# Summing each unit's products three units behind its scan, and a convolution in two halves of 64 columns

## The chip, the cores and the metric

The kernel runs on one core of one Trainium2 chip. The metric is the device time of one launch in microseconds (us); the time given for a kernel is the median of its runs. The core has five engines that run side by side and wait for each other through semaphores: TensorE (PE; its weight loads are shown apart, as PEld), VectorE (DVE), ScalarE (ACT), GpSimd (POOL) and SyncE (SP), which here issues the DMAs.

## The reference

Four layers of a selective scan over images, each added to its input, `x = x + layer(_gn(x))`. `_gn` normalises groups of three channels. x has 8 images of 48 x 48 pixels and 96 channels. A layer, cut to what matters:

```python
xz = x @ in_proj_w.T                                   # 96 -> 2 x 192 channels
xc, z = jnp.split(xz, 2, axis=-1)
xc = conv 3x3, each of the 192 channels alone; xc = silu(xc + conv_b)
xs = [xc by rows, xc by columns, both of them backwards]          # K = 4 directions
dts, Bs, Cs = split(einsum('bkdl,kcd->bkcl', xs, x_proj_w))       # Bs, Cs: 16 states
delta = softplus(einsum('bkrl,kdr->bkdl', dts, dt_proj_w) + bias)
def step(h, inp):                                      # over the 2304 pixels
    h = exp(delta * A) * h + (delta * u) * B           # h: 192 channels x 16 states
    y = sum over states of h * C
y = sum of the four directions + D * xs; y = layernorm(y) * silu(z)
return y @ out_proj_w.T
```

Layers 0, 1 and 2 are of this form. Layer 3 writes the same recurrence with cumulative sums and a division by the decay; the kernel shortens it to the ends of each direction as long as the decay has died out, and a check at the end decides whether it must be done in full.

## The kernel before

**Work and order.** The images are taken in four pairs, layer after layer, so there are 16 passes (layer l, pair p). The 192 channels of two images make three tiles of 128 partitions (t = 0 and 1: 128 channels of one image; t = 2: the last 64 channels of both). In layers 0 to 2 a pass has 12 groups (tile, row or column order `ph`, direction `d`), each group three scans of 768 pixels (class `Chunk`, lines 684 to 875), each scan 16 *units*. Unit n takes two states (n // 2 and n // 2 + 8) of 64 channels at once, 128 partitions. That makes 3 x 4 x 12 x 3 x 16 = 6912 units. Layer 3 uses class `Edge` (lines 877 to 995), four units to a group, four states to a unit, 192 pixels: 192 units.

**A unit of layers 0 to 2.** Its steps, with the engines:

- `load` (743): SP loads C's two rows into a `cb` buffer [128, 768], spread over 64 partitions each (`fetch`, 718, DMA at line 724); at n = 0 also `brow`, the B rows in bf16 (749).
- `decay` (756, `exp` at 761): ACT makes exp(delta x A) into a `da` tile (line 764).
- `spread` (769): PE spreads B from `brow` over the partitions into the PSUM tile `b` (line 667), of which there are two buffers (`pb`).
- `scan` (786): DVE multiplies b by du (line 794) and runs the recurrence (line 798); POOL multiplies the C buffer by the result (line 807).
- In six units of 16 (n = 2, 5, 7, 10, 13, 15, `pooled`, 709) B is loaded by DMA into a `bb` buffer (`load_b`, 731) and multiplied by du on POOL (`weigh`, line 741); ACT then writes the decay into the PSUM tile `b` (764 by way of line 777).
- `add_up` (844): PE adds the products over the states into the PSUM accumulator `acc` (line 854, weights `twin`, two halves of 64 columns). A call for unit n treats one half of the pixels of the pair of units it belongs to; with the second half the two cb buffers come free. At n = 1 `begin_sum` (825) starts the accumulator (line 839, from the y so far); the last call, `add_up(NS)` from `rest_of_sum` (1194), comes with the first unit of the next scan and hands `collect` (863) to a list, which the next unit carries out: ACT copies acc to y (line 871).

**What sets the order.** `run` (1170) writes the order out by hand: for unit k it calls `get_ready(k + 1)` (1199), which issues `load_b` for k + 5, `load` for k + 4, `spread` for k + 1, `weigh` and `decay` for k + 3; then the scan of k; then `add_up` for k - LAG, with LAG = 2 (line 1167), the lag of the sum behind the scan. `keep_order` (1156) fixes that order on every engine for layers 0 to 2. Beside it run side tasks, one step per unit (`beside`, 1264): `coming` (`prepare`, 580: delta and delta x u for the next scan: lines 603, 611 to 617, 623, `to_twins` with ACT copies at 578, the DVE product at 631 or 634), and either `behind` (`epilogue`, 998, of the pass before) or `ahead` (`prologue`, 287, of the next pass). In the unit where the lagging sum is at n = 0 (`ends`, 1270) no step of `behind` or `ahead` is taken. `ahead` begins at unit LAG of a pass (1239).

**The prologue** normalises, projects the input (line 404 for 128 channels, 413 for the other 64), and convolves (`convolve`, 302): for each of 5 chunks of up to 480 pixels nine matmuls of a diagonal 128 x 128 weight `diag` with the shifted, padded image `pad` (line 312) into one PSUM bank, then an ACT copy (320). A step is one of the nine matmuls. There are 16 x 3 x 5 x 9 = 2160 of these. An f32 matmul stands as two records (two passes) in the trace.

**Constants.** `cst` [128, 352] holds the identity, a 128 x 128 block of 1/192 (`mean_w`) and the group matrix; ACT negates `mean_w` into `off` (line 173).

Of the kernel before, what the change touches and what calls it, by code (L numbers as in the profile page):

```python
# [39 lines left out]
F32 = mybir.dt.float32  # L40
BF16 = mybir.dt.bfloat16
AF = mybir.ActivationFunctionType
# [7 lines left out]
P = 128  # L50
NB, H, W, DM = 8, 48, 48, 96
L = H * W
DIN = 192
# [50 lines left out]
def ss2d_layers_kernel(ctx: ExitStack, tc: tile.TileContext, x_in, consts, weights, out):  # L104
    nc = tc.nc

    cpool = ctx.enter_context(tc.tile_pool(name="const", bufs=1))
# [3 lines left out]
    ddpool = ctx.enter_context(tc.tile_pool(name="dd", bufs=2))  # L111
    ypool = ctx.enter_context(tc.tile_pool(name="y", bufs=1))
    rpool = ctx.enter_context(tc.tile_pool(name="brow", bufs=2))
    cbpool = ctx.enter_context(tc.tile_pool(name="cb", bufs=9))
    bbpool = ctx.enter_context(tc.tile_pool(name="bb", bufs=3))
    apool = ctx.enter_context(tc.tile_pool(name="da", bufs=4))
    capool = ctx.enter_context(tc.tile_pool(name="carry", bufs=2))
# [8 lines left out]


    nc.scalar.preload_act_table_set("natural_log_exp_and_others")
    cst = cpool.tile([P, 2 * P + DM], F32, name="cst")
    nc.sync.dma_start(cst, consts)  # L130
    ident = cst[:, 0:P]
    mean_w = cst[:, P : 2 * P]
    group_w = cst[0:DM, 2 * P : 2 * P + DM]
    ones = cpool.tile([P, 1], F32, name="ones")
    nc.gpsimd.memset(ones, 1.0)
    minus = cpool.tile([P, 1], F32, name="minus")
# [33 lines left out]


    off = cpool.tile([P, P], F32, name="off")
    nc.scalar.activation(off, mean_w, AF.Copy, scale=-1.0)
    off_2 = cpool.tile([P, 2, P], F32, name="off_2")
    off_22 = cpool.tile([P, P], F32, name="off_22")
    for b in range(2):
# [91 lines left out]
    def silu(o, i, **kw):  # L268

        with tc.issue_after(nc.scalar.activation(o, i, AF.Silu, **kw).ins):  # L270
            nc.scalar.preload_act_table_set("natural_log_exp_and_others")

    def bank():
        return psum.tile([P, BANK], F32, name="ps", tag="ps")
# [8 lines left out]


    GATED, READY = "gated", "ready"

    def prologue(l, p, short=False, first=False):
        ly = layers[l]
# [13 lines left out]
        def convolve(pad, t):  # L302

            while place["tiles"] < t and not first:
                yield GATED
            u[t] = upool.tile([P, L], F32, name=f"u_{l}_{p}_{t}", tag="u")
            for c0, m in CHUNKS:
                r0, nr = c0 // W, m // W
                ps = bank()
                for j in range(9):  # L310
                    dy, dx = divmod(j, 3)
                    nc.tensor.matmul(  # L312
                        ps[:, :m],
                        ly.diag[:, int(t == 2), j, :],
                        pad[:, r0 + dy : r0 + dy + nr, dx : dx + W],
                        start=(j == 0),
                        stop=(j == 8),
                    )
                    yield True
                nc.scalar.activation(  # L320
                    u[t][:, c0 : c0 + m], ps[:, :m], AF.Identity, bias=ly.column(t, C_CONVB)
                )
                yield
            silu(u[t], u[t])
            yield
# [6 lines left out]
        for b in range(2):  # L332
            x = tmp.tile([DM, L], F32, name=f"x_{l}_{p}_{b}", tag="tmp")
            if l == 0:
# [14 lines left out]
                for i, (c0, m) in enumerate(CHUNKS):  # L349
                    q, ld = m // 4, loaded[i]  # L350
                    ps = bank()
# [27 lines left out]
            ps = bank()  # L379
# [8 lines left out]
            ps = bank()  # L388
            nc.tensor.matmul(ps[0:DM, 0:1], group_w, dv, start=True, stop=True)
            yield True  # L390
            scale, shift = gn[:, b, 0:1], gn[:, b, 1:2]
# [6 lines left out]
            pad = padded(f"pad_{l}_{p}_{b}")  # L398
            q0 = 64 * b
            for c0, m in CHUNKS:  # L400
                r0, nr = c0 // W, m // W
                rows = slice(1 + r0, 1 + r0 + nr)
                ps = bank()
                nc.tensor.matmul(
                    ps[:, :m], ly.inw[:, 0:P], x[:, c0 : c0 + m], start=True, stop=True
                )
                yield True
                nc.scalar.copy(
                    pad[:, rows, 1 : W + 1], ps[:, :m].rearrange("p (r w) -> p r w", w=W)
                )  # L410
                yield
                ps = bank()
                nc.tensor.matmul(
                    ps[q0 : q0 + 64, :m], ly.inw[:, P:DIN], x[:, c0 : c0 + m], start=True, stop=True
                )
                yield True
                nc.scalar.copy(
                    pad2[q0 : q0 + 64, rows, 1 : W + 1],
                    ps[q0 : q0 + 64, :m].rearrange("p (r w) -> p r w", w=W),
                )  # L420
                yield
# [742 lines left out]
                last[i.engine] = i.name  # L1164

    groups = [(t, ph, d) for t in range(3) for ph in range(2) for d in range(2)]
    LAG = 2
    LOADS, DECAYS = 3, 2

    def run(pairs, short):  # L1170
# [58 lines left out]
        for k, ((l, p, unit), c, n) in enumerate(todo):  # L1229
# [7 lines left out]
            if done:  # L1237
                behind, done = Side(epilogue(*done), 195), None
            if unit == LAG and following:
                ahead = Side(begin(*following), 300)  # L1240
# [28 lines left out]

            ends = l not in short and k > LAG and todo[k - LAG][2] == 0  # L1270
            if busy and l not in short:
                beside()
            if k >= LAG:
                (bl, bp, _), b, bn = todo[k - LAG]
                rest_of_sum(k - LAG)
                if bl in short:
                    collected()
                b.add_up(bn)
                if k > LAG and todo[k - LAG - 1][0][:2] != (bl, bp):
                    done = todo[k - LAG - 1][0][:2]  # L1280
# [20 lines left out]
    ps = bank()  # L1301
# [100 lines left out]
```

## Time and profile before

| what | value |
|---|---|
| median of 3 runs | 20514.42 us (20494.02 to 20516.52) |
| the profiled execution | 20509.65 us, span 20507.7 us |
| busy share PE, PEld, DVE, ACT, POOL | 84%, 37%, 86%, 79%, 87% |
| mean granted PE clock | 0.904 |
| POOL product L807, mean of one | 1.817 us and 1.815 us |
| DVE scan L798, mean of one | 1.739 to 1.814 us by form |
| DVE product L794, mean of one | 0.946 us |
| PE sum L854, busy in all | 7018.1 us in 27648 records |
| PE convolution L312, busy in all | 2165.7 us in 4320 records |

How to read it: "busy" is the time in which an engine executed something. A group's row names the line, the engine, the operation, what it writes and reads, the shape, the count, then busy time, mean duration of one in ns, and the engine's idle time just before these instructions with what ended it. The list of waits says which engine and line waited for which, in total, how often, and the longest. In the timeline a row is a run of like instructions: start, length, engine, line; a matmul's end is modelled, so the next row's start tells more than its length. The granted clock of PE is a share of full speed.

### The profile page before, as it was taken

Reading aid. Unit: us, or ns where it says so; the run is one execution under the profiler, and the core shown is the slowest. Engines: PE = TensorE matmul, PEld = TensorE weight load, DVE = VectorE, ACT = ScalarE, POOL = GpSimd, SP = SyncE. Lnnn points to the kernel's source line nnn. Section 1 sums busy time; section 2 is a strip of 40 time slices with the busy share of each in tenths; the row PEclk is TensorE's granted clock in tenths of the full one; section 3 lists DMA queues with packets and bytes.
Section 4 is the critical chain, followed back from the end, with each engine's and each line's share of the span. In section 5 each row is a group of like instructions: output and inputs, shape, how many; then the busy total and the mean of one; then the engine's idle time right before and its main releaser. Section 6 shows DMA issues by size and latency. Waiting matters only on the chain. (4 is left out here: it accounts for less than half of the span.)

```text
span 20507.7 us, 304889 instructions
## 1 busy us (share of the span) xinstructions
PE 17283.2 (84%) x88322; PEld 7546.6 (37%) x88322; DVE 17656.0 (86%) x14161; ACT 16243.7 (79%) x30020; POOL 17768.2 (87%) x10121
## 2 busy tenths in 40 slices
PE   8888888888888888888888888888888888888886
PEld 2323333333333333333333333333333333335565
DVE  5999999999999999999999999989989989995543
ACT  5777887887887887887877887877877877877776
POOL 5999999999999999999999999999999999995432
PEclk8998998998998999998998999988988998999997
DMA  5888888888888888888888888888888888883221
GB/s 147 223 221 222 219 220 224 222 219 221 220 225 222 219 229 221 221 229 219 221 228 220 217 225 219 218 218 220 217 219 219 220 219 222 219 220 109 76 72 51
DMA packets 1963444, 4200.13 MB, mean 205 GB/s; under 512 B 369456, under 2 KB 720048, under 8 KB 1948592
## 3 DMA queue, kind: packets, MB, share of 16 engines
q1 hardware_dynamic: 1961776, 4180.52, 77.8%
q8 instruction: 726, 11.89, 0.3%
q14 instruction: 942, 7.72, 0.2%
HBM read 4026.64 MB, written 152.27 MB: 204 GB/s over the span
## 5 line engine op out<-in xcount | busy, mean ns | idle before, releaser
L807 POOL TENSOR_TENSOR cb<-cb,da 128x768 f32<-128x768 f32 x4320 | 7831.3, 1817 | 799.5 <-issue 258.3
L854 PE MATMUL acc<-cb,twin 128*64 128x384 f32 x27648 | 7018.1, 542 | 663.6 <-POOL cb L807 660.3
L798 DVE TENSOR_TENSOR_SCAN da<-da,carry,b 128x768 f32<-128x768 f32 x2880 | 5223.3, 1814 | 176.4 <-ACT b L764 2.3
L741 POOL TENSOR_TENSOR bb<-bb,du 128x768 f32<-128x768 f32 x2592 | 4714.0, 1819 | 361.0 <-DMA bb<-xd 207.8
L794 DVE TENSOR_TENSOR b<-du,b 128x768 f32<-128x768 f32 x4320 | 4087.6, 946 | 883.9 <-PE b L667 785.4
L807 POOL TENSOR_TENSOR cb<-cb,bb 128x768 f32<-128x768 f32 x2592 | 4705.1, 1815 | 155.0 <-DVE bb L798 57.1
L667 PE MATMUL b<-brow,pick 96*64 96x512 bf16 (+2 forms) x18816 | 2761.6, 355 | 1787.6 <-DVE da L798 1408.4
L764 ACT ACTIVATE da<-dl,a 128x768 f32<-128x768 f32 x4320 | 4013.6, 931 | 245.8 <-POOL cb L807 214.0
L854 PEld LDWEIGHTS acc<-cb,twin 128*64 128x64 f32 x27648 | 2268.9, 150 | 3089.4 <-issue 1400.3
L798 DVE TENSOR_TENSOR_SCAN bb<-b,carry,bb 128x768 f32<-128x768 f32 x1728 | 3109.0, 1799 | 114.8 <-ACT b L764 53.5
L764 ACT ACTIVATE b<-dl,a 128x768 f32<-128x768 f32 x2592 | 2334.4, 901 | 590.2 <-DVE da L798 558.4
L798 DVE TENSOR_TENSOR_SCAN da<-da,b 128x768 f32<-128x768 f32 x1440 | 2525.4, 1754 | 85.6 <-DVE b L794 0.9
L667 PEld LDWEIGHTS <-pick 96*64 96x64 bf16 x18816 | 974.1, 114 | 4192.1 <-DVE da L798 2506.3
L578 ACT COPY dl<-ps 64x384 f32<-64x384 f32 x3456 | 1635.3, 473 | 756.7 <-PE ps L623 720.7
L312 PE MATMUL ps<-pad,diag 128*128 128x480 f32 (+1 forms) x4320 | 2165.7, 599 | 11.5 <-DVE eyc L1087 9.9
L623 PE MATMUL ps<-du,cst 128*64 128x384 f32 (+1 forms) x7296 | 1709.7, 516 | 93.1 <-ACT du L617 77.0
L578 ACT COPY du<-ps 64x384 f32<-64x384 f32 x3456 | 1635.7, 473 | 190.0 <-DVE ps L634 91.2
L798 DVE TENSOR_TENSOR_SCAN bb<-b,bb 128x768 f32<-128x768 f32 x864 | 1502.2, 1739 | 94.9 <-ACT b L764 40.5
L623 PE MATMUL ps<-dl,cst 128*64 128x384 f32 (+1 forms) x7296 | 1412.4, 483 | 0.0
L312 PEld LDWEIGHTS ps<-pad,diag 128*128 128x128 f32 x4320 | 687.5, 191 | 1211.4 <-issue 1090.1
L603 PE MATMUL ps<-dts,w 6*128 6x384 f32 (+5 forms) x2432 | 946.3, 595 | 176.1 <-DMA dts<-xd 103.7
L611 ACT ACTIVATE du<-ps,w 128x384 f32<-128x384 f32 (+1 forms) x912 | 521.4, 572 | 622.3 <-PE ps L603 611.5
(144 smaller groups left out, 19159.8 us busy)
## 6 DMA issues: line engine op xcount, KB each, us to landing
cb<-xd SPq DMA_DIRECT2D x13952, 192.0 KB
bb<-xd SPq DMA_DIRECT2D x5184, 192.0 KB
brow<-xb SPq DMA_DIRECT2D x864, 72.0 KB
yd<-y SPq DMA_DIRECT2D x48, 1152.0 KB
ey<-yd SPq DMA_DIRECT2D x256, 216.0 KB
cb<-xd SPq DMA_DIRECT2D x128, 384.0 KB
ex<-xs SPq DMA_DIRECT2D x256, 108.0 KB
xd<-xt SPq DMA_DIRECT2D x32, 684.0 KB
```

The costliest lines, as they stand in the source:

```text
L312: nc.tensor.matmul(ps[:, :m], ly.diag[:, int(t == 2), j, :], pad[:, r0 + dy : r0 + dy + nr, dx : dx + W], start=(j == 0), stop=(j == 8),)
L578: nc.scalar.copy(z[64 * h : 64 * h + 64, g, at], v[64 * g : 64 * g + 64])
L603: nc.tensor.matmul(o[:, :m], ly.dtw[q0 : q0 + r, k, chans], dts[q0 : q0 + r, at], start=True, stop=True,)
L611: nc.scalar.activation(e, v, AF.Abs, bias=bias)
L623: nc.tensor.matmul(v[half], ident[:, half], z1, start=(i == 0), stop=(i == 3))
L667: nc.tensor.matmul(o[64 * h : 64 * h + 64], pick[:, b, n : n + 1].to_broadcast([2 * NR, 64]), rows, start=True, stop=True,)
L741: nc.gpsimd.tensor_mul(b, b, self.du[n % 2])
L764: nc.scalar.activation(da, self.dl[n % 2], AF.Exp, scale=layers[self.l].a2[:, int(self.t == 2), n % 2, k, i : i + 1],)
L794: nc.vector.tensor_mul(b, self.du[n % 2], b)
L798: nc.vector.tensor_tensor_scan(way(h), way(da), way(b), start, ALU.mult, ALU.add)
L807: nc.gpsimd.tensor_mul(c, c, h)
L854: nc.tensor.matmul(self.acc[64 * g : 64 * g + 64, a, : self.m // 2], twin, c[:, a, :], start=False, stop=(pair + 2 == NS and not self.turns),)
```

## The change

Three things in one diff. The sum of a unit is issued three units behind its scan instead of two (`LAG = 3`), with ten `cb` buffers instead of nine. Each convolution matmul of 128 output columns, and the input projection's, becomes two matmuls of 64 columns that write the two halves of the partitions of the same PSUM bank; a step of the convolution holds both. The constants tile loses the block of 1/192, is loaded by two DMAs, and `off` is set by a POOL memset. Everything else stands as before; lines from 286 on move down by one to three.

```diff
-    cbpool = ctx.enter_context(tc.tile_pool(name="cb", bufs=9))
+    cbpool = ctx.enter_context(tc.tile_pool(name="cb", bufs=10))
...
-    cst = cpool.tile([P, 2 * P + DM], F32, name="cst")
-    nc.sync.dma_start(cst, consts)
+    cst = cpool.tile([P, P + DM], F32, name="cst")
+    nc.sync.dma_start(cst[:, 0:P], consts[:, 0:P])
+    nc.sync.dma_start(cst[0:DM, P:], consts[0:DM, 2 * P :])
     ident = cst[:, 0:P]
-    mean_w = cst[:, P : 2 * P]
-    group_w = cst[0:DM, 2 * P : 2 * P + DM]
+    group_w = cst[0:DM, P:]
...
-    nc.scalar.activation(off, mean_w, AF.Copy, scale=-1.0)
+    nc.gpsimd.memset(off, -1.0 / DIN)
...
+    halves_of = [slice(64 * g, 64 * g + 64) for g in range(2)]
...
                 for j in range(9):
                     dy, dx = divmod(j, 3)
-                    nc.tensor.matmul(
-                        ps[:, :m],
-                        ly.diag[:, int(t == 2), j, :],
-                        pad[:, r0 + dy : r0 + dy + nr, dx : dx + W],
-                        start=(j == 0),
-                        stop=(j == 8),
-                    )
+                    for half in halves_of:
+                        nc.tensor.matmul(
+                            ps[half, :m],
+                            ly.diag[:, int(t == 2), j, half],
+                            pad[:, r0 + dy : r0 + dy + nr, dx : dx + W],
+                            start=(j == 0),
+                            stop=(j == 8),
+                        )
                     yield True
...
-                nc.tensor.matmul(
-                    ps[:, :m], ly.inw[:, 0:P], x[:, c0 : c0 + m], start=True, stop=True
-                )
+                for half in halves_of:
+                    nc.tensor.matmul(
+                        ps[half, :m], ly.inw[:, half], x[:, c0 : c0 + m], start=True, stop=True
+                    )
...
-    LAG = 2
+    LAG = 3
```

## The prediction

> **What bounds the kernel now.** I read the page's busy line first, then the stretch without the start and the short last layer, then the waits, then the order on PE. The busy line and clock row of the page:
>
> ```profile
> PE 17283.2 (84%) x88322; PEld 7546.6 (37%) x88322; DVE 17656.0 (86%) x14161; ACT 16243.7 (79%) x30020; POOL 17768.2 (87%) x10121
> ...
> PEclk8998998998998999998998999988988998999997
> ```
>
> ```profile
> 600.00:18460.00 17860.00, 15147.65 (x76202) 6204.17 (x76199) 16311.59 (x12272) 14371.34 (x26559) 16594.10 (x9416) 0.91 0.85 221
> 18460.00:20508.00 2048.00, 1653.99 (x10282) 1168.22 (x10279) 981.14 (x1609) 1503.15 (x2789) 804.23 (x480) 0.89 0.28 77
> ```
>
> The columns of the second are PE, PEld, DVE, ACT, POOL busy, clock, DMA share, GB/s. In layers 0 to 2 (first line) POOL is busy 92.9% and DVE 91.3%: two engines with nearly the same load, each feeding the other. POOL's idle time there is 17860 - 16594 = 1266 us, and no edit that leaves POOL's work as it is can gain more. The short layer 3 (second line) saturates nothing.
>
> ```profile
> L807 POOL TENSOR_TENSOR cb<-cb,da 128x768 f32<-128x768 f32 x4320 | 7831.3, 1817 | 799.5 <-issue 258.3
> ...
> L741 POOL TENSOR_TENSOR bb<-bb,du 128x768 f32<-128x768 f32 x2592 | 4714.0, 1819 | 361.0 <-DMA bb<-xd 207.8
> L794 DVE TENSOR_TENSOR b<-du,b 128x768 f32<-128x768 f32 x4320 | 4087.6, 946 | 883.9 <-PE b L667 785.4
> ```
>
> A scan of 16 units costs POOL 16 x 1.817 + 6 x 1.819 = 40.0 us; it takes 17860 / (6725/16) = 42.5 us. What POOL waits for is blurred ("issue"), so I paired each of the 6912 L807 rows with its unit's scan L798: 1042 of them came after an idle POOL and began within 0.35 us of that scan's end, 928 us in all. POOL runs dry when DVE is late, and DVE is late mostly for b:
>
> ```profile
> PE b L667 <- DVE da L798: 1408.4, 1025, 6.0
> ...
> DVE b L794 <- PE b L667: 785.4, 745, 5.9
> ...
> PE acc L854 <- POOL cb L807: 660.3, 506, 8.8
> ...
> ACT y L871 <- PE acc L854: 295.0, 276, 6.3
> ```
>
> ```profile
> SPq L724 <- PE acc L854: 2065.0, 1769, 6.1
> ```
>
> So there is a ring: PE takes its queue in order; L854, a unit's sum, waits for POOL; behind the sum of unit k-3 stands L667, which makes b for unit k+1; DVE waits for b; POOL then waits for DVE. I followed PE back from each of DVE's waits for b in layers 0 to 2 to PE's last idle time: 326 of them (366 us) start at an L854 that waits for L807, most at unit 11 of a scan, where the pooled units 7 and 10 have put POOL behind. The rest start elsewhere and pass through full stretches of PE. What fills PE there is seen in its timeline (start, length):
>
> ```profile
> 8033.08 0.54 PE L854 MATMUL acc<-cb,twin 128*64 128x384 f32 x1 [2.13 <-POOL cb L807]
> ...
> 8038.75 0.81 PE L854 MATMUL acc<-cb,twin 128*64 128x384 f32 x4
> 8039.40 1.46 PE L623 MATMUL ps<-dl,cst 128*64 128x384 f32 x8
> 8040.69 0.49 PE L667 MATMUL b<-brow,pick 96*64 96x512 bf16 x4
> 8041.01 0.81 PE L854 MATMUL acc<-cb,twin 128*64 128x384 f32 x4
> 8041.76 1.07 PE L312 MATMUL ps<-pad,diag 128*128 128x480 f32 x2
> 8042.76 0.87 PE L854 MATMUL acc<-cb,twin 128*64 128x384 f32 x4
> 8043.55 1.07 PE L312 MATMUL ps<-pad,diag 128*128 128x480 f32 x2
> ```
>
> Read starts, not lengths: L854 takes 0.65 us before a 64-column L623 but 0.75 before the 128-column convolution L312 and 0.79 between two of them; L312 itself takes 1.00.
>
> **The skill.** The Trainium skill, "TensorEngine Tiling (Array Packing)", Key Properties, says that changing the tiling mode drains TensorE and that different tiles compute in parallel. The trace agrees with both: 0.10 us appears ahead of a change of width, and eight 64-column records of 384 columns (four pairs, L623) take 1.29 us, 0.32 per pair. "TensorE: Matmul & The Clock Gate", Part 2, says that weight loads are pulled ahead while matmuls stay in order: hence the ring above. Part 1 of that page says that PE's clock halves when it has been idle for a window of about 3.4 us and returns after a busy one. The trace's clock records agree in kind: 608 stretches at half clock, 3927 us, in multiples of 3.41 us; but it drops after windows that were 40% busy too.
>
> **The change part by part.** All against the profiled execution, 20509.65 us (span 20507.7); the median of the runs, 20514.42, stands 5 us above.
>
> (1) *LAG 3.* At unit k PE now sums unit k-3, which POOL was given one unit (2.65 us) earlier. The wait of 660 us on PE mostly goes; POOL's lag behind the scan's end is 1.2 us in the median and 3.6 us at the 95th percentile. For DVE I take, wait by wait, the smaller of DVE's wait and the L854 wait at its root: 302 us. Take 300. Bounds: 0, if another buffer holds DVE back; 366, if the whole stretch goes. Ten buffers: the load issued at unit k takes the buffer of k-6 instead of k-5; in both cases the sum that frees it is issued at k-1 at the latest, so SP's loads wait no longer than before, and each add-up asks for an older product. What is late next is ACT's decay L764, which waits for POOL to free one of four da tiles (see the rivals).
>
> (2) *Convolution in pairs.* Two passes of 480 columns at 0.32 x 480/384 make 0.805 us for 1.00; the L854 ahead saves 0.10, the next one about 0.05 (a following L667 0.02). That is 0.33 us per matmul. Of 2160 matmuls 1620 (3240 rows of two passes) lie in layers 0 to 2: 535 us of PE. L404 adds 120 x 0.3 = 36. In the short layer convolutions run one after the other, where passes already start 0.403 us apart: no gain. Most of the 535 us falls where PE waits for DVE anyway (1408 us) and is worth nothing. Counting 0.33 us for each convolution in the stretch behind each of DVE's waits, never more than the wait, gives 84 us outside the waits of (1) and 60 within them. Take 100; bounds 0 and 200. The pairs double this line's rows; weight loads of 64 columns are hidden behind the pair before, as in L854. If they weren't, the first load's 0.05 us per convolution, 80 us of PE, would come back.
>
> (3) *What moves with the lag.* The end of a scan's sum, its copy L871 on ACT and the start of the next sum L839 come one unit later, and so does the unit without side work. L871 now stands at unit 4 ahead of the exp of unit 5 and of the twin copies L578 for which L631/L634 wait. 139 us of DVE's waits for L578 had an L871 before it. L871 itself waits less for POOL (93 of its 295 us have that root). Take 0; bounds 80 gained, 130 lost. Side work starts one unit later, 2.65 us of some 1530 per pair of images: nothing.
>
> (4) *Loads.* L724 waits 2065 us for sums that now end sooner. 231 us of DVE's waits go back to loads of brow and dts in the same queue. Take 40; bounds 0 (DMA engines are 85% busy there) and 150.
>
> (5) *Short layer.* 31 waits for b there (85 us) start at an L969 waiting for L962. Take 50, bounds 0 and 85. Three more sums after the last scan instead of two: about 2 us, within this.
>
> (6) *Constants.* Two loads for one and a memset for an ACT copy, at the start: within 1 us either way.
>
> Sum in layers 0 to 2: 300 + 100 + 0 + 40 = 440 us of DVE's time. POOL can use it only where it ran dry (928 of 1266 us); with two loads so alike some of the lead is given back at the next bunch of pooled units. I choose 0.8: 352. With (5): 402 us. 20509.65 - 402 = 20108, near 20110 as a median.
>
> **Rivals.** *A: POOL holds DVE by another way.* ACT's decays already wait 214 us for POOL (L764 <- L807). With DVE a unit further ahead that wait takes the place of (1). For it: POOL is at 93%. Against: the four da tiles reach back six or seven units, more than PE's four (k-3 to k+1). Then (1) is worth nothing: 0.8 x 140 + 50 = 162, 20348 us. *B: PE's clock falls, slower.* PE with less to do has more empty windows. 579 us of DVE's waits for b lie in the 3492 us of half clock of layers 0 to 2, 300 us in the other 14900: 0.166 against 0.02 per us. Each further us at half clock costs 0.146. From 2750 us more (402/0.146) the gain is gone; at 4000 more it ends at 20509 - 402 + 584 = 20691, clock near 0.81. For it: drops now follow PE's waits for DVE. Against: the columns streamed stay the same. *C: more comes through* (all of (1), 200, 80, 150 and 85, undiminished): 881 us, 19629. That pairs don't run side by side would cost 1620 x 0.8 = 1300 us of PE; the L623 rows exclude it.
>
> **Numbers.** Forecast 0.62, A 0.20, B 0.06, C 0.12. The forecast's own range is 19850 to 20300. The range to 8 in 10 takes in A and part of C: 19750 to 20430. Within 0.2% (41 us, about what a measurement here can tell from no change) lies only the crossing from A to B: 0.04, taken from both; faster 0.90, slower 0.06.
>
> **What would show it.** Right: L854's wait for L807 well under 200 us; DVE's wait for b near 350; 0.81 us from a convolution to the next start, its rows 128*64; POOL over 94% busy in layers 0 to 2; clock near 0.90. Wrong: (1), if L764's wait for L807 grows by hundreds of us; (2), if L312's pair takes 1.0 us; (3), if waits for L578 or for L871 grow; B, if the clock falls under 0.84.

## The result and the profile after

The changed kernel takes 20459.59 us, median of 19 runs (20429.11 to 20482.59); the kernel before took 20508.68 us on the same chip, median of 19 runs (20483.19 to 20536.33). The ratio is 0.9974 [0.9967, 0.9981]: faster by a quarter of a per cent, 49 us, where 402 were forecast. The direction was right, the time lies above the range, and the gain that was forecast was eight times too large. All lines below from 286 on stand one to three lower than in the kernel before: the sum is L857, B's spread L670, DVE's product L797, the scan L801, ACT's copy of the sum L874, the twin copies L581, the DVE products that wait for them L634 and L637.

First the parts that came as written. The busy line, the clock row and the groups on the page of the changed kernel (span 20442.3 us):

```profile
PE 16648.0 (81%) x92962; PEld 7367.2 (36%) x92962; DVE 17632.0 (86%) x14161; ACT 16230.7 (79%) x30009; POOL 17771.0 (87%) x10122
...
PEclk8898898898998898998898998898899888989997
...
L810 POOL TENSOR_TENSOR cb<-cb,da 128x768 f32<-128x768 f32 x4320 | 7835.6, 1819 | 778.7 <-DVE da L801 197.3
L857 PE MATMUL acc<-cb,twin 128*64 128x384 f32 x27648 | 6434.1, 548 | 64.2 <-POOL cb L810 57.5
...
L797 DVE TENSOR_TENSOR b<-du,b 128x768 f32<-128x768 f32 x4320 | 4079.1, 944 | 600.5 <-PE b L670 593.7
...
L314 PE MATMUL ps<-pad,diag 128*64 128x480 f32 (+1 forms) x8640 | 2080.9, 576 | 44.3 <-ACT du L581 29.6
```

POOL has the work it had (17771 us for 17768), at the same price. The sum's wait for POOL fell from 660.3 to 57.5 us. The convolution has twice the rows, 64 columns wide. What one costs is read from the starts in PE's timeline of the changed kernel:

```profile
8005.93 0.50 PE L670 MATMUL b<-brow,pick 96*64 96x512 bf16 x4
8006.26 0.81 PE L857 MATMUL acc<-cb,twin 128*64 128x384 f32 x4
8006.90 0.97 PE L314 MATMUL ps<-pad,diag 128*64 128x480 f32 x4
8007.71 0.81 PE L857 MATMUL acc<-cb,twin 128*64 128x384 f32 x4
8008.35 0.97 PE L314 MATMUL ps<-pad,diag 128*64 128x480 f32 x4
```

0.81 us from a convolution to the next start, and 0.64 for the sum ahead of it, where it was 0.75: on PE itself steps (1) and (2) did just what they said. Now the stretch that decides, and the short layer, by the same windows as before:

```profile
600.00:18460.00 17860.00, 14565.52 (x79632) 6076.62 (x79632) 16268.87 (x12257) 14357.61 (x26532) 16580.40 (x9407) 0.89 0.85 221
18460.00:20508.00 2048.00, 1617.03 (x11114) 1114.59 (x11114) 977.28 (x1604) 1484.81 (x2768) 796.58 (x475) 0.89 0.27 76
```

PE's busy time fell from 15148 to 14566 us, and POOL's did not move: 16580 for 16594 us, 92.8%. The engine that bounds these layers ran dry as long as before. The lists of waits, over the whole span, say through what. Three lines of before that the prediction doesn't show, then those of after:

```profile
DVE ps L631 <- ACT dl L578: 196.3, 101, 103.7
PE b L667 <- DMA brow<-xb: 178.9, 50, 8.6
DVE ps L634 <- ACT dl L578: 116.3, 115, 3.6
```

```profile
PE b L670 <- DVE da L801: 2078.7, 1605, 5.2
ACT y L874 <- PE acc L857: 732.4, 317, 5.7
DVE b L797 <- PE b L670: 593.7, 463, 4.8
...
PE b L670 <- DMA brow<-xb: 323.8, 88, 6.8
DVE ps L634 <- ACT dl L581: 295.6, 193, 87.5
...
ACT da L767 <- POOL cb L810: 285.7, 262, 3.8
DVE ps L637 <- ACT dl L581: 233.4, 198, 3.1
...
DVE bb L801 <- ACT b L767: 150.3, 95, 3.8
```

DVE's wait for b fell by 192 us. The wait of ACT's copy L874 for the sum rose from 295 to 732 us, and the waits of L634 and L637 for the twin copies from 196 and 116 to 296 and 233.

The next table cuts the profiled execution at the first scan's start and at the last scan's end of layers 0 to 2, and gives each of DVE's waits between them to its root (for b: PE followed back to its last idle time, as in the prediction). Times in us:

| | before | after | difference |
|---|---|---|---|
| up to the first scan | 205.0 | 181.8 | -23 |
| layers 0 to 2 | 18356.6 | 18370.0 | +13 |
| short layer and end | 1946.2 | 1890.4 | -56 |
| DVE's waits: b, root at a sum waiting for POOL | 366 | 2 | -364 |
| b, root at a load of brow | 148 | 264 | +116 |
| b, behind a full stretch of PE | 191 | 175 | -16 |
| L634/L637 for a twin copy | 219 | 441 | +222 |
| scan of a pooled unit, for ACT's decay | 95 | 151 | +56 |
| half clock of PE, whole span | 3927 | 4426 | +499 |

The table compares one execution of each kernel, and the 19 runs of either kernel lie some 53 us apart, so the 13 us are no difference. The gain lies outside the layers from which the forecast took 352 of its 402 us. Inside them one wait of DVE vanished and others took its time.

### The profile page after: what moved, and what is told of

It reads as the page before. It is cut to its first block, busy times and chain, and to the rows that moved or that the text cites. A ratio compares the mean times of both kernels' runs of the same rounds, so it can differ in the third digit from the quotient of the medians.

```text
span 20442.3 us, 314141 instructions
## 1 busy us (share of the span) xinstructions
PE 16648.0 (81%) x92962; PEld 7367.2 (36%) x92962; DVE 17632.0 (86%) x14161; ACT 16230.7 (79%) x30009; POOL 17771.0 (87%) x10122
## 5 line engine op out<-in xcount | busy, mean ns | idle before, releaser
L810 POOL TENSOR_TENSOR cb<-cb,da 128x768 f32<-128x768 f32 x4320 | 7835.6, 1819 | 778.7 <-DVE da L801 197.3
L857 PE MATMUL acc<-cb,twin 128*64 128x384 f32 x27648 | 6434.1, 548 | 64.2 <-POOL cb L810 57.5
L801 DVE TENSOR_TENSOR_SCAN da<-da,carry,b 128x768 f32<-128x768 f32 x2880 | 5223.0, 1814 | 175.7 <-ACT b L767 1.4
L744 POOL TENSOR_TENSOR bb<-bb,du 128x768 f32<-128x768 f32 x2592 | 4716.3, 1820 | 346.5 <-DMA bb<-xd 215.9
L810 POOL TENSOR_TENSOR cb<-cb,bb 128x768 f32<-128x768 f32 x2592 | 4711.3, 1818 | 201.5 <-DVE bb L801 67.8
L670 PE MATMUL b<-brow,pick 96*64 96x256 bf16 (+2 forms) x18816 | 2639.3, 361 | 2643.2 <-DVE da L801 2078.7
L797 DVE TENSOR_TENSOR b<-du,b 128x768 f32<-128x768 f32 x4320 | 4079.1, 944 | 600.5 <-PE b L670 593.7
L801 DVE TENSOR_TENSOR_SCAN bb<-b,carry,bb 128x768 f32<-128x768 f32 x1728 | 3109.8, 1800 | 141.8 <-ACT b L767 57.3
L857 PEld LDWEIGHTS acc<-cb,twin 128*64 128x64 f32 x27648 | 2124.8, 153 | 1933.5 <-issue 1261.5
L670 PEld LDWEIGHTS <-pick 96*64 96x64 bf16 x18816 | 953.5, 116 | 5175.2 <-DVE da L801 3480.5
L801 DVE TENSOR_TENSOR_SCAN da<-da,b 128x768 f32<-128x768 f32 x1440 | 2525.3, 1754 | 86.7 <-ACT ey L1056 0.5
L314 PE MATMUL ps<-pad,diag 128*64 128x480 f32 (+1 forms) x8640 | 2080.9, 576 | 44.3 <-ACT du L581 29.6
L581 ACT COPY dl<-ps 64x384 f32<-64x384 f32 x3456 | 1633.5, 473 | 398.1 <-PE ps L626 360.5
L581 ACT COPY du<-ps 64x384 f32<-64x384 f32 x3456 | 1633.3, 473 | 269.7 <-DVE ps L637 121.3
L801 DVE TENSOR_TENSOR_SCAN bb<-b,bb 128x768 f32<-128x768 f32 x864 | 1502.6, 1739 | 142.6 <-ACT b L767 93.0
L626 PE MATMUL ps<-du,cst 128*64 128x384 f32 (+1 forms) x7296 | 1453.3, 508 | 142.7 <-ACT du L620 128.5
L626 PE MATMUL ps<-dl,cst 128*64 128x384 f32 (+1 forms) x7296 | 1325.9, 481 | 0.0
L874 ACT COPY y<-acc 128x768 f32<-128x768 f32 x360 | 415.1, 1153 | 732.5 <-PE acc L857 732.4
```

What stands on the lines that cost most here:

```text
L314: nc.tensor.matmul(ps[half, :m], ly.diag[:, int(t == 2), j, half], pad[:, r0 + dy : r0 + dy + nr, dx : dx + W], start=(j == 0), stop=(j == 8),
L581: nc.scalar.copy(z[64 * h : 64 * h + 64, g, at], v[64 * g : 64 * g + 64])
L626: nc.tensor.matmul(v[half], ident[:, half], z1, start=(i == 0), stop=(i == 3))
L670: nc.tensor.matmul(o[64 * h : 64 * h + 64], pick[:, b, n : n + 1].to_broadcast([2 * NR, 64]), rows, start=True, stop=True,)
L744: nc.gpsimd.tensor_mul(b, b, self.du[n % 2])
L797: nc.vector.tensor_mul(b, self.du[n % 2], b)
```

## The experiments

Ratios are to the kernel before, in runs on the same chip. "Main stretch" is layers 0 to 2 of the profiled execution, cut as above: 18356.6 us before, 18370.0 after; it is read from one execution, so differences of some 30 us in it mean little. Differences in us between two medians compare runs on different chips, on which the kernel before took 20501 to 20519 us. "Twin waits" are L634's and L637's waits for the twin copies, in the main stretch. No kernel leaves out a part of the computation; those called "kept busy" add matmuls with weights of zero.

**The two parts, each alone.** The lag without the pairs is the changed kernel with this edit (and L404 likewise):

```diff
-                    for half in halves_of:
-                        nc.tensor.matmul(
-                            ps[half, :m],
-                            ly.diag[:, int(t == 2), j, half],
+                    nc.tensor.matmul(
+                        ps[:, :m],
+                        ly.diag[:, int(t == 2), j, :],
```

> The lag of three and the ten buffers alone; the convolution and the input projection again as one matmul of 128 columns. Theory M (the stall moved): with the lag the waits of DVE for b that start at the sum's wait for POOL (366 us before) vanish, but ACT's copy of the finished sum to y now stands directly ahead of the twin copies for which DVE waits at unit 5 of a scan; so these waits are over 400 us (213 before) and the time is 20470 to 20530. Theory C (the clock): the lag gains and the pairs, which leave PE more idle, give it back by a lower clock; then this kernel has a clock of 0.90 or more and is 100 us or more faster than the changed kernel (under 20360).

Measured: 20547.43 us, 1.0022 [1.0014, 1.003]. The main stretch is 18461.0 us, 104 longer than before. That is 17 us above the range of theory M; theory C is out. The waits rooted at POOL are 3 us; twin waits are 471, brow 279. The part from which the forecast took most makes the kernel slower.

The pairs without the lag:

```diff
-    cbpool = ctx.enter_context(tc.tile_pool(name="cb", bufs=10))
+    cbpool = ctx.enter_context(tc.tile_pool(name="cb", bufs=9))
...
-    LAG = 3
+    LAG = 2
```

> The pairs of 64 columns alone, lag two and nine buffers as before. Theory M: the pairs are worth their prediction or part of it, 40 to 120 us, 20390 to 20470, since nothing is put in front of ACT's twin copies; DVE's waits for b that start at the sum's wait for POOL stay near 366 us. Theory C: the clock falls to 0.89 here too, and the kernel is no faster than before (20490 to 20560).

Measured: 20427.36 us, 0.9961 [0.9948, 0.9975]; main stretch 18287.5 us, 69 shorter. The pairs bring what they were given (80), and more than the whole change does: the lag costs.

**Where the lag's gain goes: the copy L874 and delta.** The next two move either side of the pair of steps that meet on ACT. First delta's side task starts one unit later (in `prepare`), so that the twin copies again stand as far behind the copy of the sum as before:

```diff
         dts = c.dts
+        if isinstance(c, Chunk):
+            yield
```

> The changed kernel, with the preparation of the next scan's delta begun one unit later, so that the twin copies come at unit 5 and the copy of the finished sum at unit 4, as far apart as before the change. Theory M: DVE's waits for the twin copies fall from about 530 us to under 250, and the time by 150 to 300 us (20160 to 20310). Theory C: the waits may fall, but PE stays as idle and its clock as low, and the time stays within 60 us of 20460.

Measured: 20145.73 us, 0.9824 [0.981, 0.9837]; main stretch 18057.6, POOL's idle time there 1019 us for 1313. The time is 14 us below the range expected, but the twin waits only fall from 441 to 327, where under 250 were expected. Waits rooted at brow fall from 264 to 206, those of pooled scans for ACT's decays from 151 to 70.

Then the other side: the end of the sum, and with it the copy, one unit sooner, with the lag left at three. The next sum's start stays at its unit:

```diff
         def rest_of_sum(k):
-            before = todo[k - 1][1] if k > 0 else None
-            if isinstance(before, Chunk) and (k == len(todo) or todo[k][1] is not before):
-                before.add_up(NS)
+            c, n = todo[k][1:]
+            if isinstance(c, Chunk) and n == NS - 1:
+                c.add_up(NS)
...
-                rest_of_sum(k - LAG)
...
                 b.add_up(bn)
+                rest_of_sum(k - LAG)
```

> The changed kernel, with the last call of a scan's sum issued right behind the sum of unit 15, one unit sooner, so that ACT's copy of the sum comes at unit 3 as before the change while every other sum stays three units behind. The last call reads the same two products as the call before it, so it adds no wait. Theory M (the copy of the sum in front of the twin copies took the gain): waits for the twin copies fall from 441 us in layers 0 to 2 to 200 to 300 and the time by 120 to 300 us, 20160 to 20340. Rival D (it was the preparation's place that helped in the run before, not the copy's): the waits stay over 400 us and the time within 50 us of 20460.

Measured: 20280.05 us, 0.9885 [0.987, 0.9901]; main stretch 18216.1, 154 shorter than after. Twin waits are 170 us for 441, less than in the kernel before. The copy waits less for the sum. The window 600 to 18460 of the changed kernel, then of this one:

```profile
ACT y L874 <- PE acc L857: 716.4, 307, 5.7
```

```profile
ACT y L874 <- PE acc L857: 350.8, 262, 4.0
```

The edit also takes the copy out of the unit in which the next sum starts, but PE's wait for the copy there was only 49 us and falls to 17.

So most of the lag's loss hangs on where the copy stands. What happens there is seen in the timelines at a change of scan (start, length, engine, line). In the kernel before the last matmuls of the sum stand ahead of delta's:

```profile
8015.66 0.81 PE L854 MATMUL acc<-cb,twin 128*64 128x384 f32 x4
8016.31 1.46 PE L623 MATMUL ps<-du,cst 128*64 128x384 f32 x8
8016.55 0.80 ACT L871 COPY y<-acc 128x768 f32<-128x768 f32 x1 [0.68 <-PE acc L854]
...
8020.39 1.93 ACT L578 COPY dl<-ps 64x384 f32<-64x384 f32 x4
```

In the changed kernel they stand behind the first half of them:

```profile
6233.94 2.77 PE L626 MATMUL ps<-du,cst 128*64 128x384 f32 x8
...
6236.88 0.81 PE L857 MATMUL acc<-cb,twin 128*64 128x384 f32 x4
...
6237.53 1.45 PE L626 MATMUL ps<-dl,cst 128*64 128x384 f32 x8
...
6237.77 1.51 ACT L874 COPY y<-acc 128x768 f32<-128x768 f32 x1 [3.87 <-PE acc L857]
...
6239.08 0.90 ACT L767 ACTIVATE b<-dl,a 128x768 f32<-128x768 f32 x1
...
6239.98 1.92 ACT L581 COPY dl<-ps 64x384 f32<-64x384 f32 x4
...
6241.94 0.84 DVE L637 TENSOR_TENSOR ps<-ps,u 128x384 f32<-128x384 f32 x1 [1.97 <-ACT dl L581]
...
6244.62 1.81 POOL L810 TENSOR_TENSOR cb<-cb,bb 128x768 f32<-128x768 f32 x1 [1.48 <-DVE bb L801]
```

ACT stands at its copy for 3.87 us while PE, whose clock was 0.50 from 6219.5 to 6236.6, spends 2.77 us on eight records that take 1.45 at full clock two lines below. The last sum follows, the copy starts, and the twin copies stand behind it. DVE stops for 1.97 us at L637, and POOL is dry for 1.48 us two steps later. With half clock in it this is one of the longer cases: the 307 waits of this kind in the window take 2.3 us in the mean.

**Each further.** With lag 2, delta one unit later (the edit of delta above, `LAG = 2`, nine buffers):

> The control: lag two, nine buffers, pairs, and the preparation of delta one unit later. Theory M: waits for the twin copies fall below 207 us, but DVE's waits that start at the sum's wait for POOL stay over 300 us, so 20300 to 20400, 27 to 130 us faster than the pairs alone and 150 us or more slower than lag three with the same preparation (20146). Rival D: the later preparation gives it all, and this kernel reaches 20110 to 20200.

Measured: 20695.68 us, 1.009 [1.0077, 1.0104]; twin waits 886 us. Both theories are missed, by 296 us or more. The later delta is no gain by itself.

Delta later, and DVE's product L634/L637 in a step of its own after that of the twin copies:

```diff
                 c.ready = True
-                yield
+            yield
             times_u(v)
```

> Lag three, pairs, preparation one unit later, and DVE's product for the next scan one unit behind its twin copies in the first half too (as it already is in the second). Theory M: the 323 us of waits at unit 6 that remained with the preparation later go, and 80 to 220 us of it come through: 19930 to 20070. If the bank that is held a unit longer stops PE instead, 20120 to 20250.

Measured: 20183.33 us, 0.9836 [0.9823, 0.985], which misses the 19930 to 20070 expected and lies in the range of the other branch, though no run shows that the held bank is the reason. Twin waits are 328 us, no fewer than the 327 without it: nearly all of them have gone to unit 14, at the other half of delta, where ACT's wait for PE (L628) is their root.

Both edits at once, the sum's end sooner and delta later:

> Lag three, pairs, the sum's last call one unit sooner and the preparation of delta one unit later: the copy of the sum at unit 3, the twin copies at unit 5. Theory M, if it is the distance between the copy and the twin copies that counts: waits for the twin copies under 327 us and 20040 to 20140. If the distance of one unit was enough, the waits that remained have another root and the time is within 50 us of 20146. The control with lag two had this same distance and was slow (20696); if the place of the copy doesn't matter beside that, this one is slow too, over 20300.

Measured: 20508.89 us, 1.0000 [0.9992, 1.0009]; twin waits 784 us. Two edits that gain 180 and 314 us alone give a loss of 49 together. A theory by which only the distance between the copy and the twin copies counts falls here: the distance is two units here, more than in either edit alone, and the waits are the most but for the run with lag 2 and delta later, where it is two as well. The roots have changed as well. In its list of waits (window 600 to 18460) the copy hardly waits, but the twin copies wait for delta's matmuls, and DVE for them:

```profile
ACT dl L581 <- PE ps L628: 702.5, 563, 3.3
...
DVE ps L639 <- ACT dl L581: 446.9, 209, 4.8
DVE ps L636 <- ACT dl L581: 320.9, 207, 4.4
...
ACT y L876 <- PE acc L859: 76.7, 99, 2.0
```

and its timeline shows delta's matmuls L628 behind the start of the next sum, L844:

```profile
3159.32 1.48 PE L844 MATMUL acc<-y,cst 128*64 128x384 f32 x4
...
3161.27 1.46 PE L628 MATMUL ps<-dl,cst 128*64 128x384 f32 x8
...
3162.78 1.93 ACT L581 COPY dl<-ps 64x384 f32<-64x384 f32 x4 [2.28 <-PE ps L628]
...
3164.74 0.81 DVE L639 TENSOR_TENSOR ps<-ps,u 128x384 f32<-128x384 f32 x1 [3.02 <-ACT dl L581]
```

The new theory: what counts is what stands ahead of delta's matmuls in PE's queue, and of the twin copies in ACT's. The same kernel, with the side step ahead of the sum in the one unit in which the next sum starts:

```diff
-            if busy and l not in short:
+            early = l not in short and (busy or k > LAG and todo[k - LAG][2] == 1)
+            if early:
                 beside()
...
-            if not (busy and l not in short):
+            if not early:
                 beside()
```

> As the run with the sum's last call sooner and delta later (20509), but in the unit that starts the next sum the side steps come ahead of it on PE, so that delta's matmuls L626 no longer stand behind the start of the sum. Theory O (the order on PE: twin copies wait for whatever stands between them and their matmuls): waits for the twin copies fall from 784 us to under 350, 20030 to 20150. Theory M' (distance of two units is bad by itself): within 80 us of 20509.

Measured: 20125.79 us, 0.9813 [0.98, 0.9826], 383 us less than without this edit; twin waits 291 us. Its waits in the same window:

```profile
ACT dl L581 <- PE ps L628: 223.7, 252, 3.7
...
DVE ps L639 <- ACT dl L581: 149.0, 159, 4.8
DVE ps L636 <- ACT dl L581: 137.7, 174, 4.3
```

One swap on PE takes ACT's wait for delta from 702 to 224 us. The side step of `behind` or `ahead` moves along with delta's. The order on PE is shown to be the cause in that kernel.

**The lag with the copy left in place.** The lag alone, with the sum's end one unit sooner (both edits above), so that step (1) stands without step (3):

> The lag of three and ten buffers with unpaired convolution and the sum's last call one unit sooner. Lag alone was 20547, 47 us slower than before. If the copy's place is worth here what it is with the pairs (180 us), 20350 to 20390: then the lag's own worth is 120 to 160 us, less than half of the 292 forecast for it with the short layer. If lag and pairs share the gain, 20420 to 20500.

Measured: 20426.57 us, 0.9960 [0.9946, 0.9973]; main stretch 18302.2 us, 54 shorter than before. Beside the lag alone that is 121 us less in the medians, 159 in the main stretch of one execution each; the time lies in the second range, that of a shared gain. Its waits rooted at POOL are 8 us (366 before); brow 273 (148), full stretches of PE 285 (191), the pooled scan for ACT 146 (95). Twin waits are 177 (219).

**The rows of B.** brow's load in a method of its own, four units earlier and ahead of the C rows:

```diff
-        def load(self, n):
+        def load_rows(self, n):
...
+            early(LOADS + 4, "load_rows")
             early(LOADS + 1, "load_b")
```

> The changed kernel, with the bf16 rows of B (brow) loaded eight units ahead of their scan instead of four and ahead of the C rows in SP's queue. Theory M: DVE's waits for b that go back to brow (264 us after the change, 149 before) vanish and the time falls by 80 to 200 us (20260 to 20380). Theory C: no more than 40 us, since the waits of DVE at the start of a scan are set by PE at half clock.

Measured: 20398.58 us, 0.9943 [0.993, 0.9957], about 60 us less than the changed kernel. DVE's waits with their root at brow are gone (264 to 0). But scans of pooled units now wait 267 us for other things than ACT, half of it for POOL's product L744 (129 us, 30 in the changed kernel), where that class had 133 us. More than three quarters of the wait went to the next thing in line.

The same with the sum's end sooner:

> The changed kernel with the sum's last call one unit sooner (20280) and the rows of B loaded eight units ahead. If the wait for brow (301 us there) is a bound of its own, 20080 to 20180. If DVE at that point only arrives early at POOL's backlog, as the run with the rows alone suggests (60 us for 264), 20210 to 20260.

Measured: 20221.34 us, 0.9859 [0.9843, 0.9874], 59 us less than with the sooner end alone; pooled scans again wait more for other things than ACT, 276 us.

**PE's clock.** Four pairs of bf16 matmuls with weights of zero, added into `acc` at units 12, 13 and 14, leave the sums as they are and keep PE busier ahead of the change of scan. First with delta later:

```diff
+    nothing = cpool.tile([2 * NR, 64], BF16, name="nothing")
+    nc.gpsimd.memset(nothing, 0.0)
...
                 b.add_up(bn)
+                if l not in short and n in (12, 13, 14):
+                    for _ in range(4):
+                        for g in range(2):
+                            nc.tensor.matmul(
+                                b.acc[64 * g : 64 * g + 64, 0, : b.m // 2], nothing,
+                                b.brow[:, : b.m // 2], start=False, stop=False,
+                            )
```

> Lag three, pairs, preparation one unit later (20146), with four pairs of bf16 matmuls of zero weights added to the running sum at units 12, 13 and 14 of each scan, where PE has little to do and its clock drops most; the sums don't change. Theory C (the clock took part of the gain): half-clock time falls from 4136 us by 1000 or more and the time by 40 to 150 us. Theory M (the clock only follows): half-clock time may fall, the time stays within 40 us or gets longer by the added 0.64 us of PE in some units.

Measured: 20065.48 us, 0.9782 [0.9769, 0.9795], 80 less than without; half clock 3316 us for 4136, a fall of 820 where 1000 were expected.

The changed kernel kept busy:

> The changed kernel as it is, with four pairs of bf16 matmuls of zero weights added to the running sum at units 12, 13 and 14. The price of half clock from the run before (80 us for 820 us, about 0.1 us per us) says: half-clock time from 4426 us to about 3500, time 60 to 120 us lower (20340 to 20400). If the clock matters only where the twin copies don't hold, under 40 us.

Measured: 20255.79 us, 0.9876 [0.9861, 0.9891], 204 us less than the changed kernel, where 60 to 120 were expected. Half clock 3197 us for 4426. Its window of layers 0 to 2:

```profile
600.00:18460.00 17860.00, 15031.69 (x90554) 6604.39 (x90556) 16405.15 (x12427) 14494.04 (x26785) 16722.09 (x9487) 0.93 0.83 223
```

PE does 466 us more, and every other engine gets further in the same time. Twin waits stay (451): this is another cost, beside that of the copy.

And the kernel before kept busy, to see whether that cost is the change's:

> The kernel before the change with PE kept busy by zero weights at units 12 to 14. Theory K (half clock costs the changed kernel more, since there PE stands in front of the copy): 40 us or less gained here, against 204 in the changed kernel. Rival: the clock cost the kernel before as much; then 150 to 230 us faster, 20280 to 20360, and the clock explains at most the 499 us by which half-clock time grew, 60 to 80 us of time.

Measured: 20371.24 us, 0.9933 [0.992, 0.9947], half clock 2815 us for 3927, main stretch 132 shorter: 0.12 us per us. The gain of 131 us lies between what the theory (40 or less) and its rival (150 to 230) expected, nearer the rival: the kernel before paid for the half clock too. That the gain comes through the clock, and not from where the added matmuls stand in PE's queue, is argued from the fall in half clock; no run separates the two.

**Put together.** Delta later, rows earlier and kept busy:

> What has helped, together: lag three, pairs, preparation one unit later, rows of B eight units ahead, PE kept busy at units 12 to 14. If the parts add (20146 - 80 - 60), 20000 to 20020; if the rows only shift the wait, 20040 to 20080.

Measured: 20090.02 us, 0.9795 [0.9781, 0.9808], 25 us above the same without the rows, and 10 above the range for "only shift the wait": the rows bring nothing here (pooled scans wait 224 us for other things than ACT).

The sum's end sooner, kept busy:

> The changed kernel with the sum's last call one unit sooner and PE kept busy. If the copy's place and the clock are two causes that add: 20280 - 204 = 20060 to 20110. If both act on the same wait (the copy waits for PE at half clock), the second adds less than 100: 20190 to 20250.

Measured: 20103.76 us, 0.9804 [0.9791, 0.9818], 176 less than the sooner end alone, so the two add.

The mended order, kept busy:

> The run with the sum sooner, delta later and the order on PE mended (20126), with PE kept busy by zero weights at units 12 to 14. If the clock's part adds as it did in three other kernels (80 to 204 us), 19960 to 20050; if POOL now bounds, 20060 to 20110.

Measured: 20042.81 us, 0.9770 [0.9756, 0.9783]: the fastest here, 417 us below the changed kernel. Its main stretch is 17965.7 us, with POOL idle for 910 of them:

```profile
600.00:18460.00 17860.00, 15369.42 (x91904) 6901.35 (x91902) 16513.58 (x12604) 14652.44 (x27113) 16801.78 (x9535) 0.92 0.83 223
```

POOL is 94.1% busy in this window, whose last 310 us are already the short layer: what the forecast asked of the change itself.

## Why the prediction was wrong

Two steps failed: (1), in what a vanished wait is worth, and (3), which was put at nothing. That the time fell at all is no merit of the main term: the lag alone is slower by 0.2% (1.0022), and the gain is that of the pairs, the short layer and the start. For layers 0 to 2, on profiled executions, forecast with the factor 0.8:

| step | forecast | measured | from |
|---|---|---|---|
| (2) pairs | -80 | -69 | pairs alone against before |
| (1) and (4) lag and loads | -272 | -54 | lag alone with the copy in place, against before |
| (3) copy one unit later | 0 | +154 | after, against the same with the sum's end sooner |
| sum | -352 | +31 | |
| the change as a whole | -352 | +13 | |

The lag measured on top of the pairs (sooner end against pairs alone) gives -71 for the second row; the sum must then be the whole, since each row starts where the one before ended. The copy's place measured without the pairs gives +159 for the third. Each figure compares two single executions. The ratios of the whole kernels, each good to some 30 us, give -80 for the pairs, -82 for the lag with the copy in place (-156 on top of the pairs), of which some 30 to 40 are the short layer's and the start's, and +183 for the copy's place (+127 without the pairs). So the lag is worth some 50 to 115 us in layers 0 to 2, and the copy's place costs 127 to 183. The signs don't depend on the method.

**(1), the lag.** The mechanism held: the sum's wait for POOL went under 200 us as written (57.5), and 366 us of DVE's waits with that root became 2. The worth did not follow. To take, wait by wait, "the smaller of DVE's wait and the L854 wait at its root" treats each wait as if nothing else stood behind it. With the copy in place, 358 us of this root are gone from the lag alone, and 125 came back at brow, 94 as full stretches of PE, 51 at ACT's decays: 270, of 358. I had set the whole factor for what comes next at 0.8; for this term, with the loads, it was between 0.16 and 0.34 (54 to 115 of 340). That lies inside the bounds of (1), 0 to 366; the 0 was "if another buffer holds DVE back". It wasn't one buffer: a load, full stretches of PE and ACT's decays took the time. That the vanished wait turned into these is read from the sums by root; only the load has an experiment of its own, the earlier rows. The prediction's mark for success, DVE's wait for b near 350, was missed with 594.

**(2), the pairs.** Right in price (0.81 us to the next start) and in worth (69 for 80). That most of the time freed on PE is worth nothing was right too. With the pairs alone, in the window 600 to 18460, PE is busy 306 us less (14841 for 15148), and its waits for DVE (L670, 1364 to 1490) and for POOL (L857, 633 to 781) take 275 of them.

**(3), what moves with the lag.** This is the step with the wrong sign in the result. It named the right instructions and the right order ("L871 now stands at unit 4 ahead of the exp of unit 5 and of the twin copies L578"), then took 0 between 80 gained and 130 lost. Measured: 154 to 159 lost in the main stretch, 127 to 183 by the ratios: at or beyond the bound. Its own sign of being wrong, that waits for L578 or for L871 grow, came true for both. It reckoned only with the waits that already had an L871 before them. But before, the sum's end came in unit 2, where no step of `behind` or `ahead` is taken. Now unit 2 has such a step, and one more unit with delta's matmuls stands ahead of the sum's end on PE, in 51 of 359 cases wholly or in part at half clock, as in the timeline above. In the median the copy starts 8.2 us after a scan's first unit ends, for 5.2 before, and the wait of ACT at the copy rose from 295 to 732 us. The first twin copy moves from 8.6 to 10.0 us. Of the 441 us of twin waits, 350 go back to ACT waiting at this copy for PE; before these were 78 of 219, and with the sum's end sooner they are 16 of 170. Some 255 of the 350 come with no half clock in the 3 us ahead of the copy: the place is the cause, and half clock adds to it.

**(4), the loads.** Forecast 40 gained; brow's waits rose by 116 us instead. SP's loads do wait less for sums, but what remains of the time is taken by another owner. In the stretch of layers 0 to 2, SP's waits after:

```profile
SPq L727 <- PE acc L857: 1913.9, 1610, 7.3
SPq L727 <- POOL cb L810: 889.0, 1108, 2.8
```

Before, in the same stretch, these were 2169.5 and 674.8. The experiment with earlier rows says what the wait is worth: 60 of 264 us.

**(5), (6).** The short layer gave 56 us for 50. The start gave 23 that no step had: in all kernels with pairs the first scan starts at 182 to 190 us, for 205 before. The first passes' convolutions run there one after another; a stretch of them takes 35.0 us for 36.5, which explains a few us of the 23. Half clock ahead of the first scan goes with the rest: 74 us before (72 to 75 in the kernels without pairs, which start at 205 to 207), 38 after (38 to 43 in those that start at 182 to 184, 53 to 60 in those at 188 to 190). Why it is less was not traced.

**The rivals.** A did not come: ACT's decays wait 286 us for POOL, for 214. B came in part. The clock fell to 0.892, half clock grew by 499 us; at 0.12 us per us, from the kernel before kept busy, that is 60 us, which lie within the rows of the table and not beside them. The price, from main stretches, differs between the kernels that were kept busy (0.06 with delta later, 0.16 in the changed kernel, 0.18 with the sum's end sooner), so 60 may be 30 to 90. The prediction's price (0.146) was of this size, though it counted a wait as half clock when any part of it fell there; by time, 504 us of these waits lie in half clock and 379 outside, which makes 0.12. Its count, no growth, was not right. The clock is a cost of its own, which the kernel before pays as well.

Still open: why delta one unit later helps with the lag of three by more (314 us) than the sooner end (180), beyond the fewer waits of several kinds that the trace shows; the 290 us of twin waits that remain in the best kernel; and why POOL's waits at L810 that the profile puts down to a sum on PE (L857) rose from 84 to 195 us with the change, and are 38 with delta later. Taking the copy off ACT wasn't tried, nor more than ten `cb` buffers.

## What to carry to other kernels

Don't price a wait that is removed from a queue at its own length, but by what it exceeds the next waits at the same point by. In this kernel, where two engines are over 90% busy, between a sixth and a third of it came through, where four fifths were forecast; for the rows of B it was under a quarter. When a schedule step moves by one slot, look at what stands ahead of it and behind it in the new slot, on each queue that it touches, and at the speed that this engine has there; do not carry over a slack read in the old slot. Test a compound change by its parts: here one part was a gain of 0.4% and the other a loss of 0.2%, and moving one call back gave nearly four times the gain of the whole (180 us for 49).

## What the runs showed of the hardware

The Trainium skill, "TensorE: Matmul & The Clock Gate", Part 1, has the half clock come after an idle window, and tells of a kernel in which frequent short idle spells were enough. The trace of the kernel before agrees with the second. Its half clock comes in stretches of multiples of 3.41 us; cut into windows of that length, layers 0 to 2 show a drop after every full-speed window in which PE was busy under 40% (297 of 297), after 65% of those with 40 to 50%, 26% of those with 50 to 60%, and 15% of those with 60 to 70%. Nineteen of twenty returns come after a window with 87% and more. So a window need not be idle. Of the 536 drops in layers 0 to 2 of that kernel, 134 come between the start of a scan's last unit and that of the next scan's first. Matmuls with weights of zero count as work here: 24 of them per scan took 1229 us of half clock and 204 us of time from the changed kernel.

The same page, Part 2, has matmuls keep their program order on PE. The runs agree: one swap of two groups of matmuls in each scan was worth 383 us over the kernel.
